# Layer 0's projection of a graph-attention kernel: raw rows with the mean taken out of the weights, weights on another queue, a written-out VectorE order, and the first adjacency block in two transfers

## The chip, the cores and the metric

The kernel runs on one core of a Trainium2 chip. The core has five engines that run side by side and meet through semaphores: TensorE (PE, with its weight loads as PEld), VectorE (DVE), ScalarE (ACT), GpSimd (POOL) and SyncE (SP). SP, ACT and POOL issue DMA transfers, which all share the same 16 DMA engines. The metric is the device time of one execution in microseconds (us); lower is better.

## The reference, cut to what matters

Inputs are 3327 rows of 256 float32 features and a 3327 x 3327 int32 adjacency with entries 0 or 1. Two layers follow one another. In layer 0 the rows are normalised and go through graph attention with two heads, then through a mixture of 16 experts (the best two for each row). In layer 1 they go through graph attention with one head, then through 30 steps of a recurrence. Only the start of layer 0 is touched by the change in substance:

```python
def _layernorm(x, axis=-1, eps=1e-5):
    m, v = jnp.mean(x, axis, keepdims=True), jnp.var(x, axis, keepdims=True)
    return (x - m) / jnp.sqrt(v + eps)

h   = _layernorm(x)
W1h = h @ W1.T + b1;  W2h = h @ W2.T + b2;  W3h = h @ W3.T + b3      # two heads of 128 columns
s1  = einsum(W1h, a[:, :128]);  s2 = einsum(W2h, a[:, 128:])          # one number per row and head
e   = leaky_relu(s1[:, None] + s2[None, :], 0.2), minus infinity where adj is 0
x   = x + softmax(e over neighbours) @ W3h
```

Since s1 and s2 are linear in h, the kernel folds W1, W2 and a into four score columns beside the 256 columns of W3, so that one product of a row with a 256 x 260 matrix `wv` gives everything that attention needs. The products of h with `wv` can be written as (x @ wv') / std, where wv' is `wv` with the mean of each column over its 256 rows subtracted: taking the mean out of the weights does the same as taking it out of the rows, and the factor 1/std of a row can be multiplied in at the end.

## The kernel before, in words

Rows are held in 26 tiles of 128 rows; `groups` takes them four at a time (the last group has two). A tile framework (a scheduler) decides the order of the instructions on each engine from the program's order and the dependencies; instructions passed to `tc.keep_in_program_order` keep their order among themselves. DMA waits and buffer reuse become semaphores.

**Start.** SP issues the loads of x, group by group (L77). ACT's queue writes zeros into three DRAM tensors (`lists`, the last rows of `given`, `no_row`; L418 to L421). POOL's queue loads W1, W2, a, the biases and W3 (`once`, L425, and L437). When W1, W2 and a are there, TensorE folds the score columns (L440), VectorE copies them into `wv` (L444), and TensorE folds the bias of the scores (L452).

**Projection** (`project`, called at L479). For every group `normalized` takes the statistics of its tiles on VectorE (`bn_stats` L116, `bn_aggr` L117, variance plus epsilon L119), GpSimd raises it to the power of minus one half (`rstd`, L121), and VectorE writes the normalised rows `xn` (L128). For each pair of tiles TensorE transposes the four 128 x 128 blocks (L148), ScalarE copies them out of PSUM as `hT` (L149), and one pair later TensorE multiplies them with `wv` (L163, four products of 260 columns). VectorE moves each tile's result out, adding b3 (L459) and the score bias (L463). After each group ScalarE makes three exponentials of the scores and VectorE a negated copy `minus` (L195 to L198). PSUM tiles come from a ring of four banks that transposes and products share.

**Adjacency.** `take_graph` brings in a block of rows of the adjacency. A DMA on POOL's queue reads int32 from DRAM and writes bytes to a DRAM scratch `in_bytes` (L325); for each 128-row tile of it SP then issues a DMA transpose into `adjT` in SBUF (L335). `in_bytes` has room for six tiles and every block starts at its beginning, so that the next block's load waits until the transposes of the one before it are done. The first block has four tiles (`groups0[0]`) and is asked for when the statistics of the fourth group are known (`first_rows`, L473 to L477); POOL issues it behind that group's `rstd`.

**Attention** (`attend`). For one block of target rows and one head at a time, 26 steps run over the source tiles. In each step ScalarE makes `e` (L276), VectorE masks it with `adjT` to `pT` (L281), and TensorE accumulates `pT` with `wh` (L286). A step needs the adjacency of all tiles of its block, so the first step needs all four tiles of the first block. The first two passes (two heads) use 512 columns, those of the second block 768. Ahead of them TensorE spreads the row factors (`rb`, L243) and transposes them all (L224). Routing, the experts, layer 1's attention and the recurrence follow.

Of the kernel before, what the change touches and what calls it, by code (L numbers as in the profile page):

```python
# [21 lines left out]
P = 128  # L22
ALPHA = 0.2
EPS = 1e-5
# [7 lines left out]
def gat_moe_gat_recurrent_ffn(ctx: ExitStack, tc: tile.TileContext, a: dict, out: bass.AP):  # L32
# [77 lines left out]
    def inverse(src, scale=1.0):  # L110

        n = len(src)
        mv = small.tile([P, MOST, 2], F32, name="mv")
        for j in range(n):
            st = small.tile([P, 6], F32, name="st")
            nc.vector.bn_stats(st, src[j])  # L116
            nc.vector.bn_aggr(mv[:, j, :], st)  # L117
        ve = small.tile([P, MOST], F32, name="ve")
        nc.vector.tensor_scalar(ve[:, :n], mv[:, :n, 1], EPS, 1.0 / scale**2, op0=ALU.add, op1=ALU.mult)  # L119
        r = small.tile([P, MOST], F32, name="rstd")  # L120
        power = nc.gpsimd.tensor_tensor(r[:, :n], ve[:, :n], neg_half[:, :n], ALU.pow)  # L121
        return r, mv, power.ins

# [9 lines left out]
    def without_mean(wv, n_out, ones, p):  # L133

        for k in range(KD):
            nc.tensor.matmul(p[:, :n_out], lhsT=ones, rhs=wv[:, k, :], start=(k == 0), stop=(k == KD - 1))
        for k in range(KD):
            nc.vector.scalar_tensor_tensor(
                wv[:, k, :], p[:, :n_out], -1.0 / D, wv[:, k, :], op0=ALU.mult, op1=ALU.add
            )  # L140
# [11 lines left out]
    def project(groups, wv, n_out, finish, work, ps, ps_p, aside, raw=True):  # L152

        pending = None

        def products(hT, t, r):
            for j in range(2):  # L160
                p = ps_p()
                for k in range(KD):
                    nc.tensor.matmul(  # L163
                        p[:, :n_out], lhsT=hT[:, j, k, :], rhs=wv[:, k, :], start=(k == 0), stop=(k == KD - 1)
                    )
                finish(t + j, p, *([r[:, j : j + 1]] if raw else []))

        for ts in groups:
            n = len(ts)
            tiles = [x[:, t, :] for t in ts]  # L170
            if raw:
                r, _, power = inverse(tiles)
            else:
                xn = work.tile([P, G, D], F32, name="xn")
                power = normalized(tiles, [xn[:, j, :] for j in range(n)])
            aside(ts, power)
            for j0 in range(0, n, 2):
                hT = turned(x[:, ts[j0] : ts[j0] + 2, :] if raw else xn[:, j0 : j0 + 2, :], work, ps)
                if pending:
                    products(*pending)  # L180
                pending = hT, ts[j0], r[:, j0 : j0 + 2] if raw else None
        products(*pending)

    class Scores:
# [9 lines left out]
        def finish(self, t0, t1):  # L194
            nc.scalar.activation(self.full[:, t0:t1], self.s[:, t0:t1, 1], AF.Exp)  # L195
            nc.scalar.activation(self.part[:, t0:t1], self.s[:, t0:t1, 1], AF.Exp, scale=ALPHA)
            nc.scalar.activation(self.row[:, t0:t1], self.s[:, t0:t1, 0], AF.Exp, scale=1.0 - ALPHA)
            nc.vector.tensor_scalar(self.minus[:, t0:t1], self.part[:, t0:t1], -1.0, None, op0=ALU.mult)  # L198
# [111 lines left out]
    def take_graph(ts, behind):  # L310
# [6 lines left out]
        b = in_bytes  # L317
# [65 lines left out]
    with ExitStack() as moe:  # L383
# [28 lines left out]
        with ExitStack() as pre:  # L412
# [3 lines left out]
            zero = hold.tile([P, E * CAP * 2 // P], F32, name="zero")  # L416
            nc.vector.memset(zero, 0.0)
            nc.scalar.dma_start(lists.rearrange("(p n) k -> p (n k)", p=P), zero)  # L418
            for k in range(2):
                nc.scalar.dma_start(given[k * NP + N : (k + 1) * NP, :], zero[: NP - N, :D])  # L420
            nc.scalar.dma_start(no_row, zero[:2, : NP // 4])  # L421

            def once(name, shape, src):
                t = hold.tile(shape, F32, name=name)
                nc.gpsimd.dma_start(t, src)  # L425
                return t

            w1 = once("gw1", [P, H, D], a["W1"].rearrange("(h c) d -> c h d", c=P))
            w2 = once("gw2", [P, H, D], a["W2"].rearrange("(h c) d -> c h d", c=P))
            aT = once("gaT", [P, 2, H], a["aT"].rearrange("(s c) h -> c s h", c=P))  # L430
            b1 = once("gb1", [P, H], a["b1"])
            b2 = once("gb2", [P, H], a["b2"])
            b3 = once("gb3", [P, D], every_partition(a["b3"], D))
# [3 lines left out]
            nc.gpsimd.dma_start(wv[:, :, :D], a["W3T"].rearrange("(k p) c -> p k c", p=P))  # L437
            pv = bank()
            for q, (s, h, k) in enumerate((s, h, k) for s in range(2) for h in range(H) for k in range(KD)):
                nc.tensor.matmul(  # L440
                    pv[:, q : q + 1], lhsT=(w1, w2)[s][:, h, k * P : (k + 1) * P], rhs=aT[:, s, h : h + 1],
                    start=True, stop=True,
                )
            nc.vector.tensor_copy(  # L444
                wv[:, :, D:].rearrange("p k q -> p q k"), pv[:, : 2 * H * KD].rearrange("p (q k) -> p q k", k=KD)
            )
            shift = hold.tile([P, 2, H], F32, name="shift")
            nc.vector.memset(shift, 0.0)
            pv = bank()
            for h in range(H):  # L450
                for s, b in ((0, b1), (1, b2)):
                    nc.tensor.matmul(  # L452
                        pv[:, h : h + 1], lhsT=b[:, h : h + 1].to_broadcast([P, P]), rhs=aT[:, s, h : h + 1],
                        start=(s == 0), stop=(s == 1),
                    )
            nc.vector.tensor_copy(shift[:, 0, :], pv[:, :H])

            def split0(t, p):
                nc.vector.tensor_tensor(  # L459
                    wh[:, t, :, :C], p[:, :D].rearrange("p (h c) -> p h c", h=H),  # L460
                    b3.rearrange("p (h c) -> p h c", h=H), ALU.add,
                )
                nc.vector.tensor_tensor(  # L463
                    sc.s[:, t], p[:, D : D + 2 * H].rearrange("p (s h) -> p s h", h=H), shift, ALU.add
                )
                if t % G == G - 1 or t == NT - 1:
                    sc.finish(t - t % G, t + 1)

# [4 lines left out]
            def first_rows(ts, power):  # L473
                nonlocal behind
                behind = power
                if ts is groups[3]:
                    take_graph(groups0[0], behind)  # L477

            project(groups, wv, D + 2 * H, split0, work, ps, bank, first_rows, False)  # L479
# [184 lines left out]
        nc.vector.tensor_copy(vec[:, 0:1], part[:E])  # L664
# [5 lines left out]
        def find_tiles(end, s0, n):  # L670
# [40 lines left out]
            nc.vector.tensor_scalar(vec[:, 1:2], part[:E], float(CAP), None, op0=ALU.mult)  # L711
# [298 lines left out]
    with ExitStack() as st:  # L1010
# [33 lines left out]
        def split1(t, p, r):  # L1044
            nc.scalar.activation(s_wh[:, t, 0, : D + 2], p[:, : D + 2], AF.Copy, scale=r)
            for ts in groups1:
                if t == ts[-1]:
                    sc.finish(ts[0], t + 1)

# [223 lines left out]
```

## Time and profile before

| | us |
|---|---|
| median of 3 runs | 1819.82 |
| lowest, highest | 1819.78, 1823.14 |
| the profiled execution's own time | 1820.76 |
| span of that execution's trace | 1819.0 |

| engine | busy us | share of the span | instructions |
|---|---|---|---|
| PE | 1764.8 | 97% | 10768 |
| PEld | 1608.8 | 88% | 10768 |
| DVE | 1303.0 | 72% | 3861 |
| ACT | 1214.2 | 67% | 1557 |
| POOL | 916.2 | 50% | 702 |

All later readings come from the one profiled execution; its times count from the start of the span. In lines of the timeline the first number is the start, the second the duration of a merged run of equal instructions, xN their number, and the bracket is the idle time of that engine just before, with what ended it. In lines of waits the numbers are the total, how often, and the longest. float32 products appear as two records each[...], so that eight records of L163 are the four products of one pair of tiles.

### The profile page before, as it was taken

Reading aid. Unit: us, or ns where it says so; the run is one execution under the profiler, and the core shown is the slowest. Engines: PE = TensorE matmul, PEld = TensorE weight load, DVE = VectorE, ACT = ScalarE, POOL = GpSimd, SP = SyncE. Lnnn points to the kernel's source line nnn. Section 1 sums busy time; section 2 is a strip of 40 time slices with the busy share of each in tenths; the row PEclk is TensorE's granted clock in tenths of the full one; section 3 lists DMA queues with packets and bytes.
Section 4 is the critical chain, followed back from the end, with each engine's and each line's share of the span. In section 5 each row is a group of like instructions: output and inputs, shape, how many; then the busy total and the mean of one; then the engine's idle time right before and its main releaser. Section 6 shows DMA issues by size and latency. Waiting matters only on the chain.

```text
span 1819.0 us, 32184 instructions
## 1 busy us (share of the span) xinstructions
PE 1764.8 (97%) x10768; PEld 1608.8 (88%) x10768; DVE 1303.0 (72%) x3861; ACT 1214.2 (67%) x1557; POOL 916.2 (50%) x702
## 2 busy tenths in 40 slices
PE   6999999999999999799999999999999999999997
PEld 6999999899999999688888878888888888888885
DVE  7888888863222222657677678889899988998997
ACT  2877677642212121456666579999999999999993
POOL 3011212155454542101111028999999999999993
PEclk9999999999999999899999999999999999999999
DMA  8996360247796875400000038888877888878778
GB/s 174 121 126 81 78 102 10 72 161 211 239 257 192 212 205 163 154 14 18 18 21 16 12 103 188 199 195 199 198 198 192 194 194 196 198 198 201 196 191 233
DMA packets 497026, 269.75 MB, mean 148 GB/s; under 512 B 361797, under 2 KB 469116, under 8 KB 496858
## 3 DMA queue, kind: packets, MB, share of 16 engines
q1 hardware_dynamic: 478722, 229.29, 50.6%
q0 software_dynamic: 13456, 33.60, 10.7%
q10 hardware_dynamic: 4680, 4.76, 0.8%
q8 instruction: 88, 1.44, 0.3%
q14 instruction: 80, 0.66, 0.1%
HBM read 168.19 MB, written 105.58 MB: 151 GB/s over the span
## 4 chain that ended last, share of the span: by engine, by line
PE 54%; DVE 3%; DMA 1%; issue 0%; ACT 0%; SPq 0%; POOL 0%; ACTq 0%; DVEq 0%; POOLq 0%
PE po L1181 36%; PE acc L286 15%; PE bank L1145 3%; DVE pT L281 1%; PE acc L163 1%; DMA old<-kept 1%; DVE x L1030 0%; DMA given<-wh,to 0%; DMA zT<-given 0%; DVE x L1199 0%; DVE x L1191 0%; DVE st L116 0%; POOL rstd L121 0%; DVE low L1064 0%; SPq L1168 0%
## 5 line engine op out<-in xcount | busy, mean ns | idle before, releaser
L276 ACT ACTIVATE e<-rb,minus,full 128x384 f32<-128x384 f32 (+3 forms) x494 | 399.3, 823 | 167.4 <-DVE pT L281 149.6
L1181 PE MATMUL po<-wc,adjT 128*128 128x256 f32 x2144 | 480.0, 380 | 7.5 <-DMA adjT<-apart 5.5
L1115 POOL TENSOR_TENSOR th<-th,x 128x1024 f32<-128x1024 f32 (+1 forms) x210 | 464.7, 2213 | 17.4 <-ACT th L1112 15.7
L281 DVE SCALAR_TENSOR_TENSOR pT<-e,part,adjT 128x384 f32<-128x384 f32 (+3 forms) x494 | 383.5, 782 | 118.4 <-PE acc L286 102.4
L1181 PEld LDWEIGHTS po<-wc,adjT 128*128 128x128 f32 x2144 | 405.9, 191 | 63.5 <-issue 4.9
L1191 DVE SCALAR_TENSOR_TENSOR x<-po,rr,bb 128x256 f32<-128x256 f32 x780 | 323.7, 476 | 73.4 <-PE po L1181 72.8
L286 PE MATMUL acc<-wh,pT 128*128 128x129 f32 x2704 | 310.4, 276 | 2.1 <-DVE pT L281 2.1
L286 PEld LDWEIGHTS acc<-wh,pT 128*128 128x128 f32 x2704 | 305.3, 192 | 2.9 <-DVE pT L281 2.7
L286 PE MATMUL acc<-s_wh,pT 128*128 128x257 f32 x1352 | 295.5, 381 | 4.0 <-DVE pT L281 4.0
L286 PEld LDWEIGHTS acc<-s_wh,pT 128*128 128x128 f32 x1352 | 255.8, 190 | 43.1 <-DVE pT L281 7.4
L1124 DVE BATCH_NORM_STATS2 stats<-z 128x6 f32<-128x256 f32 x780 | 274.4, 412 | 1.4 <-ACT z L1119 1.4
L1156 ACT COPY adjT<-z 128x1024 int16<-128x1024 int16 x268 | 266.9, 1039 | 2.1 <-DVE pT L281 2.0
L1132 POOL TENSOR_TENSOR rr<-v,neg_half 128x4 f32<-128x4 f32 (+1 forms) x210 | 205.6, 979 | 94.2 <-DVE v L1127 88.9
L121 POOL TENSOR_TENSOR rstd<-ve,neg_half 128x4 f32<-128x4 f32 (+3 forms) x28 | 31.9, 1141 | 409.4 <-DVE ve L119 325.6
L1112 ACT ACTIVATE th<-x 128x1024 f32<-128x1024 f32 (+1 forms) x210 | 208.8, 994 | 41.5 <-DVE x L1191 37.7
L1181 PE MATMUL po<-wc,zT 128*128 128x256 f32 x976 | 220.8, 379 | 0.1
L1119 ACT ACTIVATE z<-th 128x1024 f32<-128x1024 f32 (+1 forms) x210 | 209.0, 995 | 6.5 <-POOL th L1115 6.4
L1181 PEld LDWEIGHTS po<-wc,zT 128*128 128x128 f32 x976 | 182.9, 190 | 24.0 <-DVE x L1191 0.5
L931 ACT ACTIVATE e<-bank 128x512 f32<-128x512 f32 x61 | 36.4, 597 | 239.0 <-issue 184.8
L939 DVE TENSOR_TENSOR pT<-e,bank 128x512 f32<-128x512 f32 x61 | 41.9, 687 | 180.3 <-PE bank L881 160.1
L903 POOL DMA_INDIRECT given<-wh,to x61 | 61.1, 1001 | 114.5 <-DVE wh L902 100.0
L594 POOL DMA_INDIRECT lists<-pair,ati x52 | 63.1, 1214 | 107.8 <-DVE ati L581 50.0
(204 smaller groups left out, 1648.0 us busy)
## 6 DMA issues: line engine op xcount, KB each, us to landing
apart<-adjT SPq DMA_DIRECT2D x268, 256.0 KB
wh<-in_w_dram SPq DMA_DIRECT2D x120, 512.0 KB
first_set<-in_w_dram SPq DMA_DIRECT2D x63, 512.0 KB
in_bytes<-in_adj_dram POOLq DMA_DIRECT2D x3, 2496.0 KB
asked<-e POOLq DMA_DIRECT2D x42, 128.0 KB
adjT<-apart SPq DMA_TRANSPOSE x268
x<-in_x_dram SPq DMA_DIRECT2D x6, 512.0 KB
kept<-x SPq DMA_DIRECT2D x8, 384.0 KB
```

The lines of the kernel that those rows point to most:

```text
L276: nc.scalar.activation(e[:, : n * P], rb[:, : n * P], AF.Relu, scale=sc.full[:, j, h : h + 1], bias=sc.minus[:, j, h : h + 1],)
L281: masked = nc.vector.scalar_tensor_tensor(pT[:, : n * P], e[:, : n * P], sc.part[:, j, h : h + 1], adjT[:, j // 2, ts[0] * P : (ts[-1] + 1 ...
L286: nc.tensor.matmul(po[c], lhsT=pT[:, c * P : (c + 1) * P], rhs=wh[:, j, h, :], start=(j == 0 and c % per_bank == 0), stop=(j == NT - 1), s ...
L594: put = nc.gpsimd.indirect_dma_start(out=lists, out_offset=bass.IndirectOffsetOnAxis(ap=ati[: rows(t), s, j : j + 1], axis=0), in_=pair[: ...
L1112: self.put(nc.scalar.activation(self.th, self.hs, AF.Tanh, scale=1.0 / S))
L1115: self.put(nc.gpsimd.tensor_tensor(self.th, self.th, self.hs, ALU.add))
L1119: self.put(nc.scalar.activation(self.z, self.th, AF.Silu, scale=1.0 / S))
L1124: self.put(nc.vector.bn_stats(stats[:, j, :6], self.z[:, j, :]))
L1132: nc.gpsimd.tensor_tensor(self.r[:, : self.n], self.v[:, : self.n, 1], neg_half[:, : self.n], ALU.pow)
L1156: self.put(nc.scalar.copy(parts[:, c : c + 2], halves[:, c : c + 2]))
L1181: nc.tensor.matmul(self.po[:, j, :], lhsT=self.zT(j, k), rhs=wc[:, k, :], start=(k == 0), stop=(k == KD - 1),)
L1191: nc.vector.scalar_tensor_tensor(self.hs[:, j, :], self.po[:, j, :], self.r[:, j : j + 1], bb, op0=ALU.mult, op1=ALU.add)
```

## The change

- `project` transposes x itself for layer 0 too; `xn` and its 26 instructions (L128) are gone. The mean is taken out of `wv` (`without_mean`: two products with a matrix of ones, two VectorE instructions). The exit of each tile multiplies by `rstd` and adds b3 or the score bias in one instruction each.
- The statistics become a generator, `inverting`, that yields after each tile. Group 0 is measured first, then come the score columns, and between their two parts the first two tiles of group 1. All later groups are measured one tile after each exit. The VectorE instructions of this stage are kept in program order.
- ACT's queue loads a, W1, W2 and W3 as its first four transfers. POOL's queue keeps b1, b2 and b3. The zeros go to SP's queue, behind the loads of x.
- TensorE begins with eight products of ones that nobody reads (`idle`).
- The first adjacency block is asked for when group 2's statistics are known, as two loads of two tiles, each with its own place in `in_bytes` and its own two transposes. POOL's small loads and index patterns (`gate_w`, `gate_b`, the iotas) come ahead of it in POOL's order; in the kernel before they came behind it.
- `minus` is made by a separate `negate`, two tiles after the group's end; two small copies of the routing (`vec`) are kept in program order. In the later stages the built programs differ otherwise only in the places of small statistics on VectorE and of two small products.

In the changed program's order TensorE runs: the eight idle products, the transposes of pair 0, the score columns, the products with ones, the bias products, the transposes of pair 1, then the products of pair 0, the transposes of pair 2, and so on. On VectorE group 2's last statistics and its variance stand behind the exit of the fifth tile.

```diff
-    def project(groups, wv, n_out, finish, work, ps, ps_p, aside, raw=True):
+    def project(groups, wv, n_out, finish, work, ps, ps_p, aside, prepare=None):
...
-                finish(t + j, p, *([r[:, j : j + 1]] if raw else []))
+                finish(t + j, p, r[:, j : j + 1])
+                next(ahead, None)
...
+        for g, ts in enumerate(groups):
+            if g == 0 or not prepare:
+                for _ in measure(ts):
+                    pass
+            r = ready.popleft()
+            for j0 in range(0, len(ts), 2):
+                hT = turned(x[:, ts[j0] : ts[j0] + 2, :], work, ps)
                 if pending:
                     products(*pending)
+                elif prepare:
+                    next(prepare)
+                    for j, _ in enumerate(measure(groups[1])):
+                        if j == 1:
+                            next(prepare)
+                    ahead = measure_all(groups[2:])
+                pending = hT, ts[j0], r[:, j0 : j0 + 2]
...
-    def take_graph(ts, behind):
+    def take_graph(ts, behind, base=0):
-        b = in_bytes
+        b = in_bytes[base * P : (base + len(ts)) * P, :]
...
+            aT = once(nc.scalar, "gaT", [P, 2, H], a["aT"].rearrange("(s c) h -> c s h", c=P))
+            w1 = once(nc.scalar, "gw1", [P, H, D], a["W1"].rearrange("(h c) d -> c h d", c=P))
+            w2 = once(nc.scalar, "gw2", [P, H, D], a["W2"].rearrange("(h c) d -> c h d", c=P))
...
+            nc.scalar.dma_start(wv[:, :, :D], a["W3T"].rearrange("(k p) c -> p k c", p=P))
...
+            idle = bank()
+            for _ in range(8):
+                nc.tensor.matmul(idle[:, :P], lhsT=ones, rhs=ones, start=True, stop=True)
...
+                without_mean(wv, D + 2 * H, ones, bank(), tc.keep_in_program_order)
...
-                nc.vector.tensor_tensor(
-                    wh[:, t, :, :C], p[:, :D].rearrange("p (h c) -> p h c", h=H),
-                    b3.rearrange("p (h c) -> p h c", h=H), ALU.add,
-                )
+                tc.keep_in_program_order(
+                    nc.vector.scalar_tensor_tensor(
+                        wh[:, t, :, :C], p[:, :D].rearrange("p (h c) -> p h c", h=H), r,
+                        b3.rearrange("p (h c) -> p h c", h=H), op0=ALU.mult, op1=ALU.add,
+                    )
+                )
...
-                if ts is groups[3]:
-                    take_graph(groups0[0], behind)
+                if ts is groups[2]:
+                    for t in groups0[0][::2]:
+                        behind = take_graph(range(t, t + 2), behind, t)
```

## The prediction, on record before the changed kernel ran

> **What bounds the kernel now.** I read the page first: PE is busy 97% of the span, so what counts is the time in which it stands still. The waits of the first 60 us say where; the timeline of that stretch says when; the DMA view gives the adjacency's pace; the table of stages says who is full.
>
> ```profile
> PE 1764.8 (97%) x10768; PEld 1608.8 (88%) x10768; DVE 1303.0 (72%) x3861; ACT 1214.2 (67%) x1557; POOL 916.2 (50%) x702
> PE bank L440 <- DMA gaT<-in_aT_dram: 12.0, 1, 12.0
> POOL in_bytes L325 <- DMA adjT<-in_bytes: 17.0, 1, 17.0
> ```
>
> PE does nothing for 12 us until W1, W2 and a have landed through POOL's queue.
>
> ```profile
> 12.04 3.54 PE L440 MATMUL bank<-gaT,gw 128*128 128x1 f32 x16 [12.04 <-DMA gaT<-in_aT_dram]
> 16.61 1.01 POOL L121 TENSOR_TENSOR rstd<-ve,neg_half 128x4 f32<-128x4 f32 x1 [0.63 <-DVE ve L119]
> 17.17 1.05 DVE L128 TENSOR_SCALAR xn<-x,mv,rstd 128x256 f32<-128x256 f32 x3
> 17.57 0.92 POOL L325 DMA_DIRECT2D in_bytes<-in_adj_dram  x1
> 20.59 3.56 PE L163 MATMUL bank<-wv,hT 128*128 128x260 f32 x8
> 24.42 1.92 PE L163 MATMUL bank<-wv,hT 128*128 128x260 f32 x8
> 46.35 3.67 PE L163 MATMUL bank<-wv,hT 128*128 128x260 f32 x16
> 48.24 0.77 POOL L325 DMA_DIRECT2D in_bytes<-in_adj_dram  x1 [16.95 <-DMA adjT<-in_bytes]
> 51.16 2.22 PE L243 MATMUL bank<-ident,row 128*128 128x128 f32 x18
> 53.30 2.95 PE L286 MATMUL acc<-wh,pT 128*128 128x129 f32 x24
> ```
>
> The first xn starts at 17.17 although its rstd was there at 8.0, because VectorE ran the statistics of later groups first. Products run from 20.59 to 50.02, a pair every 2.19 us once under way; the first pT follows at 52.50. Beside this chain runs another: the adjacency, asked for at 17.57. The next load of in_bytes may start only when its transposes are done, so 48.24 is the latest moment at which it was there: 30.7 us after the request, and 4.3 us before it was needed. That slack limits the change.
>
> ```profile
> 20.60:50.00 29.40, 29.40 (x151) 25.39 (x151) 21.97 (x97) 8.95 (x30) 4.68 (x14) 1.00 0.85 116
> 52.50:101.80 49.30, 49.30 (x442) 49.18 (x442) 43.07 (x65) 45.96 (x60) 0.69 (x1) 1.00 0.94 116
> ```
>
> PE is full in both stages (first figure behind the length), so a microsecond won or lost before the first pT should reach the end.
>
> **The change part by part.**
>
> *Weights on ACT's queue.* Before, ACT's queue waited for the memset of the zeros until 2.36. Now it can begin with SP, at 0.8. x shows the delay: issued at 0.80, 0.52 MB moved by 4.0, first statistics at 4.72. The three matrices are 0.77 MB. x moves in 2 KB packets, rows of the weights are 1 KB; if the queues take turns by packet, the weights get a third of some 345 GB/s from about 2.9 on: W2 is complete after 1.57 MB, at 7.5, W3 after 2.36 MB, at 9.7; with 0.6 for the landing 8.1 and 10.3. Against 12.04 that is the first gain. x itself gets no more and no fewer bytes to share with, and the zeros behind it on SP delay only the transposes, which are far later. POOL's three small loads have no work behind them that is late.
>
> *Until the first product.* Idle products, transposes of pair 0 and the W1 columns fit before 8.1. Eight W2 records at 0.22 (3.54/16) end by 9.9; the copy, ready by 10.3, does not bind. The products with ones: layer 1's same step takes 1.15 from its first product (728.44) to its first correction on VectorE (729.59), so 10.4 to 11.5; the two corrections take 0.77 (there 0.76). Meanwhile PE does eight bias records (at 0.11, the spacing of L243 and L286, to 12.4) and pair 1's transposes (0.60). First product: 13.0, 7.6 earlier than 20.59. Bounds: 12 if W3 gets an equal share, 15.5 if PE is still slow (below).
>
> *Projection.* Transposes and products stay; xn goes (26 instructions by 0.35 on VectorE, which is not the bound). The exit is one instruction with a scalar more; L138 (the same kind, from PSUM) takes 0.42, L459 0.42: nothing. VectorE per pair: two exits 0.83, two statistics 0.82, some 0.2 of small ones: 1.85 below PE's 2.19, so the written order fits; a statistic stands in front of an exit for 0.4, which the four banks cover. PE's stage is 29.43 less the slow start (3.56 - 1.92 = 1.64): 27.8. It ends at 40.8, and with before's tail of 2.48 the first pT could come at 43.3.
>
> *The adjacency's request* does not come earlier. It waits for group 2's rstd, which in VectorE's new order stands behind the fifth tile's exit. Fifth product: 2 x 2.19 + 0.81 = 5.2 after the first one, wait and exit 0.6, statistics and variance 0.3, handover 0.15, power 1.01: 7.3. Request at 20.3, against 17.57. POOL has nothing else waiting there: the small loads and iotas moved ahead of it took 18.48 to 21.8 in before and now lie between two powers, from about 8 on.
>
> *Two halves.* In before: request to first bytes 1.6, load 16.8 (19.2 to 36), landing and start of the transposes 2.7, transposes 38.7 to 47.2, landing about 1. The transposes' work, by their share of the engines:
>
> ```profile
> q1 hardware_dynamic: 1781, 0.45, 49.9%
> q1 hardware_dynamic: 3478, 0.87, 109.5%
> q1 hardware_dynamic: 1525, 0.38, 53.3%
> ```
>
> (three windows of 4 us, 37 to 49) is 2.0 + 4.4 + 2.1 = 8.5 us of all engines. While the load runs its queue holds 103 to 104% of them, so the trace has no idle engine under which half one's transposes could vanish. [...] By that rule the sum stays 1.6 + 16.8 + 8.5 + 1 = 28: only the gap of 2.7 is filled. By a hope that they overlap fully it would be 26.4; if halves share evenly and the gap opens again behind half two, 30.7. I take 28. The adjacency is there at 48.3.
>
> *First pT*: the later of 43.3 and 48.3, plus 0.1: 48.4 against 52.50. **Gain 4.1 us.** The next load is asked for at the same time as before (48.3 to 48.24), so its transposes end near 92.2 as before, while its first use moves from 101.8 to 97.7: covered, by 5.5. The later blocks have more.
>
> *A new idle stretch on PE.* After products end at 40.8 the row factors take 3.4 more as before (50.02 to 53.38), to 44.2; the first attention product comes at 49.2. PE, which went without a break, now idles for 5 us. What that costs is seen elsewhere:
>
> ```profile
> 739.29 1.12 PE L148 MATMUL bank<-ident,x 128*128 128x128 f32 x4 [7.76 <-DVE x L1030]
> 741.12 3.38 PE L163 MATMUL acc<-wv,hT 128*128 128x258 f32 x8 [0.72 <-ACT hT L149]
> 745.62 2.45 PE L163 MATMUL acc<-wv,hT 128*128 128x258 f32 x10 [0.24 <-ACT hT L149]
> ```
>
> After 7.76 idle the same products take almost double for about 5 us (3.38 for eight against 1.92: 1.5, and 0.5 in the transposes: 2.0 lost). After 1.82 idle (L136 at 728.44) they ran at full pace. The granted clock in the table is 1.00 throughout and doesn't show it. [...] I take nothing for the number, 2.0 for the range.
>
> **The sum.** Profiled execution: 1820.76 (span 1819.0 and 1.76 around it), less 4.1: 1816.7. The median of the runs lies 0.94 below that execution, so 1815.7.
>
> **Rivals.**
> - *Half speed after the idle stretch.* As above, with 2.0 back: gain 2.1, 1817.7. For it: the 7.76 row; against it: the stretch is shorter.
> - *The overlap is better, or the start is earlier.* W3 by 9.3 puts the request at 19.3; transposes hidden: 26.4 and pT at 45.8. Gain 6.7, 1813.1; with no adjacency wait at all 52.5 - 43.3 = 9.2, 1810.6. Against it: the load's 103%.
> - *Late request, slower than before.* If the idle products fail to bring PE to speed (16 records of L440 in a row, 12.04 to 15.58, did not; L163 at 20.59 was still slow), the products with ones, the bias and pair 1's transposes double: first product at 15.5, the first eight products and the transposes cost 1.7 more, request at 24.5. With halves that share evenly, 30.7 more: 55.2, first pT 2.8 later than before, and a slow restart adds 2.0: 4.8 slower, 1824.6. It decides from a request at 52.4 - 28 = 24.4 on, or 21.7 with even sharing. Against it: idle products and transposes keep PE busy from 1.5 to about 7.
> - *The change does nothing for the time*: products earlier, the adjacency again at 50 to 52: gain under 2, 1818.8.
>
> **How the numbers follow.** About 0.2% (3.6 us) is what a measurement of this kernel can tell from no change; the three runs differ by 3.4. Main case 0.42 (its own range 2.6 to 5.6, two thirds above 3.6); half speed 0.25; better overlap 0.20; nothing 0.06; slower 0.07. Faster by over 0.2%: 0.28 + 0.20 = 0.48; slower 0.07; within 0.45. The range leaves out the ends of the second and third rival: 1811.6 to 1821.0.
>
> **What would show it.** In the changed profile: first product near 13, request near 20.3 as two L358 issues, transposes of half one in the queue before half two has landed, the last pair near 40.8, first pT at 48.4 with a wait on a DMA of adjT, and behind it PE records of L319 at 0.11 or 0.22. Wrong if the request comes before 18 or after 23, if the wait before the first pT is on anything but the adjacency, or if the second block's first step waits.

## The result and the profile after

The changed kernel takes 1829.41 us (median of 6 runs, 1828.87 to 1832.61) where the kernel before took 1820.16 in the same session (6 runs, 1819.13 to 1823.14): ratio 1.0041, 95% interval 1.0029 to 1.0054. It is slower by 0.4%; the forecast was 1815.7, and the range ended at 1821.0. The profiled execution of the changed kernel took 1829.29, with a span of 1827.6.

The waits of its first 60 us, in the columns used above (total, times, longest):

```profile
PE bank L475 <- DMA gw<-in_W_dram: 3.9, 2, 2.3
DVE pT L314 <- DMA adjT<-in_bytes: 6.4, 1, 6.4
PE acc L319 <- DVE pT L314: 5.4, 1, 5.4
```

The 12 us in which PE waited for the weights have become two waits of 3.9 together, as the change wants. But 6.4 us of waiting for the adjacency have appeared ahead of the first pT, where there was none. The timeline says how:

```profile
7.68 1.02 PE L475 MATMUL bank<-gaT,gw 128*128 128x1 f32 x8 [1.59 <-DMA gw<-in_W_dram]
11.05 1.86 PE L475 MATMUL bank<-gaT,gw 128*128 128x1 f32 x8 [2.35 <-DMA gw<-in_W_dram]
15.44 1.71 PE L490 MATMUL bank<-gaT,gb 128*128 128x1 f32 x8
17.89 3.67 PE L178 MATMUL bank<-wv,hT 128*128 128x260 f32 x8
27.87 1.22 POOL L358 DMA_DIRECT2D in_bytes<-in_adj_dram  x2
44.51 3.67 PE L178 MATMUL bank<-wv,hT 128*128 128x260 f32 x16
56.30 2.08 DVE L314 SCALAR_TENSOR_TENSOR pT<-e,part,adjT 128x512 f32<-128x512 f32 x3 [6.37 <-DMA adjT<-in_bytes]
56.45 0.75 POOL L358 DMA_DIRECT2D in_bytes<-in_adj_dram  x1 [13.46 <-DMA adjT<-in_bytes]
```

The first product comes at 17.89, only 2.7 us before 20.59. The request for the adjacency goes out at 27.87 instead of 17.57: 10.3 later. From it to the adjacency, for which the first pT at 56.30 waited, it takes 28.4 us; in the kernel before it was 30.7, read at the next load of in_bytes. So the adjacency is 8.1 later than before; 4.3 us of that was slack, and the first pT is 3.8 later (56.30 against 52.50), although the last products end 1.8 earlier.

The table of stretches (length; PE busy; then the other engines; granted clock third from the end, DMA share next to last):

```profile
8.00:12.00 4.00, 1.65 (x12) 1.57 (x11) 0.00 (x0) 0.00 (x0) 3.08 (x18) 0.66 0.94 335
12.00:24.00 12.00, 11.34 (x40) 9.77 (x40) 5.25 (x21) 1.17 (x2) 1.03 (x1) 0.54 0.41 133
24.00:47.70 23.70, 23.70 (x130) 20.65 (x129) 20.05 (x88) 7.78 (x28) 5.92 (x7) 1.00 0.82 82
57.00:62.00 5.00, 4.89 (x29) 4.89 (x30) 3.10 (x6) 3.37 (x5) 0.20 (x1) 0.65 0.87 81
```

Between 8 and 12 PE works 1.65 us and loses its clock (0.66 there, 0.50 from 9.3 to 22.9 us); from 12 to 24 it is busy 11.34 of 12 us at about half speed (the same step of PE, eight bias records, takes 1.71 here and 0.95 in the run below that keeps PE at full clock). Behind the wait for the adjacency the clock is low once more (0.65). Instruction by instruction against the kernel before, attention's first product is 3.8 us late, and the products once attention is under way are 5.4 late: this restart costs another 1.6.

### The profile page after: what moved, and what is told of

Read it like the earlier page. It is cut to its first block, busy times and chain, and to the rows that moved or that the text cites. A ratio compares the mean times of both kernels' runs of the same rounds, so it can differ in the third digit from the quotient of the medians.

```text
span 1827.6 us, 32199 instructions
## 1 busy us (share of the span) xinstructions
PE 1775.2 (97%) x10788; PEld 1618.8 (89%) x10788; DVE 1298.2 (71%) x3837; ACT 1215.2 (66%) x1557; POOL 912.0 (50%) x699
## 4 chain that ended last, share of the span: by engine, by line
PE 80%; DVE 6%; DMA 6%; issue 4%; POOL 2%; ACT 1%; SPq 1%; ACTq 0%; DVEq 0%; POOLq 0%
PE po L1239 35%; PE acc L319 28%; PE bank L938 7%; PE acc L955 3%; DVE pT L314 3%; PE bank L1203 3%; DMA given<-wh,to 2%; PE acc L178 1%; PE bank L163 1%; DMA wh<-in_w_dram 1%; DMA in_bytes<-in_adj_dram 1%; PE bank L583 1%; POOL given L960 1%; DMA old<-kept 1%; SPq L368 1%
## 5 line engine op out<-in xcount | busy, mean ns | idle before, releaser
L319 PEld LDWEIGHTS acc<-s_wh,pT 128*128 128x128 f32 x1352 | 257.0, 191 | 43.6 <-DVE pT L314 7.3
```

Of the source, the lines that this page charges most:

```text
L319: nc.tensor.matmul(po[c], lhsT=pT[:, c * P : (c + 1) * P], rhs=wh[:, j, h, :], start=(j == 0 and c % per_bank == 0), stop=(j == NT - 1), s ...
```

## The experiments

Every run is compared with the kernel before, timed beside it on the same chip; its median there was 1824.8, 1826.4, 1824.8 and 1820.8 in the four sessions, so that differences count and absolute times do not. The first product is that of `wv`, the request is the first adjacency load on POOL's queue, the first pT is the first masked tile of attention; all three, in us, come from one profile of each run. "Start" is how much later than in the first profile of the kernel before PE works once attention is under way (at 100 us); it holds the first pT and the restart. In the two other profiles of the kernel before it is -0.3 and +0.4. A half-clock stretch is one in which the granted clock of the profile reads 0.50.

| kernel | first product | request | first pT | start | median less before's |
|---|---|---|---|---|---|
| before | 20.59 | 17.57 | 52.50 | 0 | 0 |
| changed | 17.89 | 27.87 | 56.30 | +5.4 | +9.3 |
| changed, again | 17.63 | 27.52 | 55.38 | +4.5 | +7.0 |
| request one group earlier | 17.53 | 19.20 | 49.83 | -2.7 | +0.6 |
| PE kept busy before attention | 17.56 | 26.93 | 54.61 | +1.9 | +6.0 |
| PE kept busy at the start | 16.04 | 23.52 | 51.45 | +1.5 | +3.1 |
| weights on SP | 16.64 | 25.21 | 53.62 | +3.7 | +5.9 |
| weights on SP, request earlier | 16.55 | 18.23 | 47.96 | -4.5 | +0.5 |
| b3 behind x | 17.27 | 26.01 | 54.12 | +4.3 | +7.9 |
| one request | 17.61 | 26.57 | 58.52 | +8.7 | +10.4 |
| norms in old order | 18.07 | 26.54 | 54.75 | +4.9 | +7.0 |
| all together | 14.23 | 16.32 | 48.38 | -4.1 | -4.4 |
| all together, again | 13.99 | 16.07 | 45.63 | -6.9 | -2.9 |
| ... with the changed norm order | 13.42 | 15.51 | 44.89 | -7.6 | -4.6 |
| ... with b3 behind group 1 | 14.14 | 16.23 | 44.36 | -8.1 | -5.8 |
| ... and vec free | 14.23 | 16.32 | 44.46 | -8.0 | -5.2 |

**Is the late request the cause?** In the changed kernel only the place of the request moves:

```diff
-                if ts is groups[2]:
+                if ts is groups[1]:
```

> The changed kernel, with the adjacency asked for behind the variance power of group 1 instead of group 2; nothing else moves. Late-request theory (the request at 27.87 us, behind the fifth tile's exit, used up the 4.3 us of slack): request near 19.7 us, adjacency there 28.4 us later at 48.1, first pT then bound by the products' end (48.2 + 2.5) at about 50.8 instead of 56.30, no cold start of PE behind it, time 1818 to 1821 us, about 8 to 10 us below the changed kernel. Rival, the halves cost: request to adjacency stays above 31 us and the first pT comes after 52.5. Rival, raw projection and the written order cost later on: first pT earlier as said, but the end no more than 3 us below the changed kernel.

```profile
19.20 1.22 POOL L358 DMA_DIRECT2D in_bytes<-in_adj_dram  x2
46.45 0.75 POOL L358 DMA_DIRECT2D in_bytes<-in_adj_dram  x1 [4.25 <-DMA adjT<-in_bytes]
49.83 12.65 DVE L314 SCALAR_TENSOR_TENSOR pT<-e,part,adjT 128x512 f32<-128x512 f32 x15 [0.68 <-ACT e L309]
```

The adjacency is there 27.3 us after the request, and pT waits for ACT, not for a DMA. Request, first pT and the missing restart came as the late-request theory said: where the changed kernel loses 7 to 9 us to the kernel before, this one loses 0.6 (ratio 1.0005, 0.9995 to 1.0015). So neither the halves nor the written order is the main loss. But the start is now 2.7 us early and the end is not; some 3 us are lost behind it.

**What is the restart worth?** 20 idle products between the projection and the row factors:

```diff
+            idle = bank()
+            for _ in range(20):
+                nc.tensor.matmul(idle[:, :P], lhsT=ones, rhs=ones, start=True, stop=True)
```

> The changed kernel with 20 further idle products of ones by ones on PE (about 4.4 us) between the last layer-0 product and the row factors; their result is used nowhere. They fill most of the 5.45 us in which PE waits for the adjacency. Theory of the clock: first pT stays at 56.3, granted clock behind it 1.00 instead of 0.63, first 768-column pT at about 105.6 instead of 107.23, time about 1.6 us below the changed kernel (1827.8). Rival, the first products there are slow for lack of pT and not for the clock: nothing changes (1829.4).

```profile
47.08 4.63 PE L531 MATMUL bank<-ones 128*128 128x128 f32 x40
55.42 8.75 PE L319 MATMUL acc<-wh,pT 128*128 128x129 f32 x76 [0.48 <-DVE pT L314]
```

```profile
55.40:60.00 4.60, 4.58 (x41) 4.58 (x42) 4.17 (x6) 4.49 (x7) 0.11 (x1) 1.00 0.85 80
```

The clock behind the wait is 1.00 instead of 0.65, and PE goes from 2.1 us late at its first attention product to 1.9 once under way, where the changed kernel goes from 3.8 to 5.4. In the runs that kept the wait the restart took 1.6 (both profiles of the changed kernel) to 2.7 us. (The first pT is 1.7 earlier than expected; 0.9 of this is the request, which was that much earlier in this execution.) The times are too close for a verdict on 1.6 us: 1.0034 (1.0022 to 1.0047).

**Why was the first product so late?** Two candidates: PE's clock, and the weights' landing. First 22 more idle products in the gaps ahead of the first real ones:

```diff
+                fill(6)                                  # ahead of W1's columns
...
+                    if (s, h, k) == (1, 0, 0):
+                        fill(11)                         # between W1's and W2's
...
+                fill(5)                                  # ahead of the products with ones
```

> The changed kernel with 22 more idle products of ones by ones on PE: 6 ahead of the columns of W1, 11 between those of W1 and W2, 5 ahead of the products of ones by W3. Theory that of the 4.9 us by which the first product missed its forecast (17.89 against 13.0) about 2 are PE's half clock and 3 the late landing of W2: W2's columns begin at 11.05 as before, the step after them runs at full pace (bias 0.85 instead of 1.71, first eight products 1.92 instead of 3.67), first product 15.5 to 16, request 25.0 to 25.5 instead of 27.87, first pT 53.5, time 2.5 to 3 us below the changed kernel. Rival, the clock does not follow from the gaps: first product 17.9, nothing changes.

```profile
11.87 0.95 PE L482 MATMUL bank<-gaT,gw 128*128 128x1 f32 x8
14.75 0.95 PE L498 MATMUL bank<-gaT,gb 128*128 128x1 f32 x8
16.04 1.92 PE L178 MATMUL bank<-wv,hT 128*128 128x260 f32 x8
23.52 1.22 POOL L358 DMA_DIRECT2D in_bytes<-in_adj_dram  x2
51.45 2.08 DVE L314 SCALAR_TENSOR_TENSOR pT<-e,part,adjT 128x512 f32<-128x512 f32 x3 [5.87 <-DMA adjT<-in_bytes]
```

```profile
8.00:12.00 4.00, 3.56 (x32) 3.59 (x33) 0.00 (x0) 0.00 (x0) 3.18 (x18) 1.00 1.04 369
12.00:16.00 4.00, 4.00 (x35) 3.88 (x34) 1.93 (x8) 0.00 (x0) 0.00 (x0) 1.00 1.07 344
```

With the clock at 1.00 the way from W2's columns to the first product takes 4.2 us instead of 6.8, and from the first product to the request 7.5 instead of 10.0. The fillers themselves hold W2's columns back by 0.8. The request gains 4 us where 2.5 had been expected, and the time follows: 3.1 above before, against 7.0 for the changed kernel on the same chip. That chip's run of it:

> The changed kernel unaltered, to be compared in one session with the experiments beside it and with the kernel before. It should again lie about 0.4% above the kernel before. Theory of a clock grid (a PE gap of some 1.9 us costs one stretch of 3.4 us at half clock when it falls wholly into one stretch of a grid that is not tied to the program's start): first pT within 0.5 us of 56.3 as before, but the single half-clock stretches (at 347.2, 736.3 and 784.1 in the first profile) at other places. Rival, these stretches belong to the program: the same stretches again.

It gave 1.0045 (1.0028 to 1.0061) and a first pT at 55.38, 0.9 from that of the first run where 0.5 had been expected; of the single half-clock stretches named, those at 347.2 and 736.3 were missing and that at layer 1's attention came again (790.5); what the profiles show around such stretches stands in the last section.

Then the landing. Weights behind x's first group on SP's queue:

```diff
-    for ts in groups:
+    for ts in groups[:1]:
...
+            for ts in groups[1:]:                        # behind aT, W1, W2, W3, all on nc.sync
```

> The changed kernel with aT, W1, W2 and W3 moved from ACT's queue to SP's, behind x's first group and ahead of its others, so that they no longer share with all of x. Theory that the weights' late arrival let PE lose its clock and so moved every later step: W2 there by 7 us instead of 11.05, first product near 12 instead of 17.89, granted clock 1.00 from 8 to 24, request near 20 to 21, first pT 48 to 49 instead of 56.3, time 1816 to 1819 us. Rival, VectorE's written order alone sets the request (statistics of groups 1 and 2 then wait for x): first product earlier, request not before 25, first pT above 53, time 1825 or more.

W1's columns ran at 6.34, but W2's still at 10.15 and the clock was lost all the same (the eight bias records took 1.71 once more); first product 16.64, request 25.21. A miss: the queue alone wins 1 us. With the earlier request too:

> Both edits together: weights on SP's queue behind x's first group, adjacency asked for behind group 1's power. If the two causes add: first product near 12, request near 15, adjacency there at 43.5, products end near 40, first pT at about 43.6, time 1811 to 1815 us, below the kernel before (1820). If the load of the adjacency now starves x and delays the later groups: last product after 44 and first pT after 47.

First product (16.55) and end of the last products (45.52) are again later than expected, and the first pT is at 47.96, not 43.6, with the adjacency there since 45.57. These are the numbers of the rival, but not its cause: from the first product to the end of the last one it takes 29.0 us here and 28.9 in the run before, whose request came 7 us later, so the early load starves nobody; the products end late because they begin late. The time stays at 1.0002 (0.9994 to 1.0010) of that of the kernel before.

What else was on the DMA engines while W2 was late? Queues in the changed kernel from 7 to 9 us (packets, MB, share of 16 engines; q10 carries the weights, q0 POOL's small loads, q1 SP's x):

```profile
q0 software_dynamic: 63, 0.13, 51.2%
q1 hardware_dynamic: 109, 0.22, 32.3%
q10 hardware_dynamic: 107, 0.11, 15.6%
```

Half of the engines' time went to b3, one row of 1 KB copied to every partition: 32 packets of 0.51 us each on average in this profile (0.28 us, and 33.5% of the engines, in the second profile of the same kernel). Moved behind x:

```diff
-            b3 = once(nc.gpsimd, "gb3", [P, D], every_partition(a["b3"], D))
+            b3 = once(nc.sync, "gb3", [P, D], every_partition(a["b3"], D))
```

> The changed kernel with only the load of b3 (one row of 1 KB written to every partition, 32 packets of about 0.5 us) moved from POOL's queue to SP's, behind x. Theory that these packets held half of the engines from 7 to 9 us in front of W2 and x: W2's columns begin at about 10 instead of 11.05, first product about 1 us earlier (16.9), request 1 us earlier (26.9), first pT 55.3. Rival, the weights are late because they share with x, and b3 is nothing: W2 at 11.

```profile
q1 hardware_dynamic: 224, 0.43, 59.4%
q10 hardware_dynamic: 219, 0.21, 34.8%
q0 software_dynamic: 26, 0.00, 1.4%
```

In the same two microseconds twice the bytes of weights and x move, and W2's last packet is there at 9.36 instead of 10.05. Yet W2's columns run at 10.70, only 0.35 earlier (in the six profiles with the changed kernel's start they run between 10.84 and 11.20): b3 was worth about a third of what was expected. Its ratio, 1.0049 (1.0031 to 1.0067), is that of the changed kernel.

**The two halves.** The first adjacency in one request at the same place:

```diff
-                    for t in groups0[0][::2]:
-                        behind = take_graph(range(t, t + 2), behind, t)
+                    behind = take_graph(groups0[0], behind)
```

> The changed kernel with the first adjacency asked for whole, in one request at the same place, instead of in two halves. Request at 27.5 to 27.9 us as in the changed kernel. If the halves are worth what the prediction took for them (they fill the gap of 2.7 us between load and transposes): adjacency there 30.7 us after the request instead of 28.0 to 28.4, first pT 58.4 to 58.8 instead of 55.4 to 56.3. Rival, the halves cost time, since the second half waits behind the first one's transposes: request to adjacency under 28 us.

```profile
26.57 0.71 POOL L358 DMA_DIRECT2D in_bytes<-in_adj_dram  x1
58.52 2.08 DVE L314 SCALAR_TENSOR_TENSOR pT<-e,part,adjT 128x512 f32<-128x512 f32 x3 [9.90 <-DMA adjT<-in_bytes]
```

From the request to the first pT 31.9 us, against 27.7 to 28.4 with halves in all the kernels of the table that waited for it. The halves are worth at least 3.5 us here (the single request of the kernel before took 30.0 to 30.7 us in its three profiles), and are no part of the loss. They do not work by overlap: from 42 to 46 us in the changed kernel the load (q0) fills the engines, and the transposes of half one (q1) get what is left. So the gap that they fill is what remains; it was 2.7 us in the kernel before, and where the rest of the 3.5 comes from is not shown.

```profile
q0 software_dynamic: 127, 0.42, 100.7%
q1 hardware_dynamic: 100, 0.03, 4.4%
```

**The loss behind the start.** Over the table the end is on average 2.8 us later than the start tells (from 0.3 less to 5.0 more). Two parts of the change also move VectorE's order behind layer 0: `inverting` sets each tile's aggregate behind the next tile's statistics, in every layer norm, and two writes of `vec` in the gate are held in program order. The norms first:

> The changed kernel with every layer norm outside layer 0's projection given back its old order on VectorE (aggregate of a tile directly behind its statistics, instead of one tile later). Theory that the new order costs about 0.44 us at the end of the first attention (five statistics instead of four behind the last row, a PE gap of 1.86 instead of 1.42 us) and a few tenths more behind it: first pT unchanged at 55.4 to 56.3, PE gap near 345 back at 1.42, time 0.5 to 1 us below the changed kernel, too little for the comparison of times to show. Rival: gap stays 1.86.

The gap stayed at 1.85: the rival. Then everything together, to see whether a clean start reaches the end:

> What the other runs found, put together: weights on SP's queue behind x's first group; b3 behind x; 17 more idle products on PE ahead of the first real ones; adjacency asked for behind group 1's power; layer norms in their old order. Expected: first product 13.5 to 14.5, no half clock at the start, request 15 to 16, adjacency there at 43.5 to 44.5, last product at 43.5 to 44.5, first pT near 45.5 to 46.5 without a long PE gap ahead of it, 6 to 7 us earlier than in the kernel before (52.5), time 3 to 6 us below the kernel before. If a gain at the start does not reach the end (as in the two runs with an early request): within 1 us of the kernel before.

```profile
14.23 1.92 PE L181 MATMUL bank<-wv,hT 128*128 128x260 f32 x8
19.48 1.12 PE L181 MATMUL bank<-wv,hT 128*128 128x260 f32 x4 [2.02 <-DVE s L518]
```

```profile
18.72 0.49 DVE L512 SCALAR_TENSOR_TENSOR wh<-bank,rstd,gb 128x256 f32<-128x256 f32 x1 [3.48 <-DMA gb<-in_b_dram]
```

Faster than before: 0.9970 (0.9961 to 0.9979). The expectation missed one thing: the first exit waited 3.5 us for b3, now too late; PE stood 2.0 us and lost its clock once more (0.79 from 16 to 24). Three variants follow, beside a second run of it:

> The version with everything together, unaltered, as the reference of the three beside it. Again about 0.3% below the kernel before (ratio 0.997), first pT at 48.4, with the PE gap of 2.0 us near 17.5 where the first exit waits for b3.

It gave 0.9985 (0.9974 to 0.9996), 1.5 us less of a gain for the same kernel; the gap was 1.19 this time, no half-clock stretch followed, and the first pT came at 45.63. With the changed order of the norms:

> The same, but with the changed kernel's order of statistics and aggregates in every layer norm. In the runs so far the end was about 3 us later than the start of attention accounts for where this order was in (seven kernels), and about 0 where it was not (two). If the order costs that: about 3 us above the version together, with no single place in the trace that takes it. Rival, those 3 us are the scatter of the executions: no difference beyond 1 us.

0.9977 (0.9967 to 0.9988), 1.7 us below the run beside it: the order of the norms does not cost the 3 us. With b3 earlier:

> The version together, with b3 moved on SP's queue from behind all of x to behind x's second group. The first exit no longer waits for it: the PE gap of 2.0 us near 17.5 goes and the half-clock stretch behind it (20.7 to 24.1) as well, last product 2 to 3.5 us earlier, first pT at 45 to 46.4 instead of 48.4, time 2 to 3 us below the version together. Rival: b3's slow packets in front of x delay group 2's statistics, and the gain is under 1 us.

```profile
14.14 1.92 PE L181 MATMUL bank<-wv,hT 128*128 128x260 f32 x8
16.23 1.22 POOL L361 DMA_DIRECT2D in_bytes<-in_adj_dram  x2
43.78 0.75 POOL L361 DMA_DIRECT2D in_bytes<-in_adj_dram  x1 [7.05 <-DMA adjT<-in_bytes]
44.36 18.01 DVE L317 SCALAR_TENSOR_TENSOR pT<-e,part,adjT 128x512 f32<-128x512 f32 x21 [0.68 <-ACT e L312]
```

PE's wait for b3 and the half-clock stretch behind it are gone: 0.9971 (0.9961 to 0.9980), 5.8 us below the kernel before, with the first pT 8.1 earlier. Its median is the lowest; those of the variant before it and of the next lie within 1.2 us of it, less than the intervals tell apart. Last, with `vec` free as well:

> As with b3 earlier, and the two writes of vec in the gate no longer held in program order, so that VectorE's order behind layer 0's projection is the one of the kernel before throughout. PE gap near 336 to 340 at 1.42 instead of 1.85 us, 0.4 us on the path; with it one fewer chance of a half-clock stretch there (1.7 us in the runs that had one). Time 0.4 to 1.5 us below the run with b3 earlier. Rival: gap still 1.85, no difference.

In the profile of the version with b3 earlier, and then in that with vec free:

```profile
332.93 3.08 PE L322 MATMUL acc<-wh,pT 128*128 128x129 f32 x16 [1.86 <-DVE pT L317]
```

```profile
332.98 2.05 PE L322 MATMUL acc<-wh,pT 128*128 128x129 f32 x16 [1.41 <-DVE pT L317]
```

So the held `vec` moves a set of statistics from under PE's work to the end of the first attention: 0.44 us, and here a half-clock stretch on top. Such a stretch followed this gap in 8 of the 14 changed profiles that had it, and costs half a microsecond more, not 1.7, since it takes the place of PE's next wait of 1.08 us: from this gap to the one of 0.69 us behind it that every profile has, it takes 13.5 us in the first of these two profiles, 12.5 in the second, and 13.0 with the gap but no stretch (the second run of everything together). In the times it does not show: 0.9972 (0.9959 to 0.9984).

Is the rest inside the first attention too? From 100 us to its last product the changed kernel and the experiments on it (ten profiles) are 0.5 to 3.4 us slower than the first profile of the kernel before, the five profiles of everything together and its variants 0.0 to 1.0. Beside `vec` and its stretch the traces show another half-clock stretch near 350 to 356 us in two of the ten (1.65 us), and a wait of PE of some 0.3 us near 370 in seven. Two more profiles of the kernel before show what moves by itself:

> The kernel before unaltered, for a second profile beside those of the experiments. First pT near 52.5. Clock grid theory: layer 1's projection start is slow again (the gap of 7.76 us holds two whole stretches), and the gap of 1.89 us before layer 1's attention (774.3) has about an even chance of a half-clock stretch, which would add 1.7 us. Rival: no half-clock stretch there in the kernel before, whatever the run.

> The kernel before unaltered, a third profile of it, on the chip of the runs beside it. Start phase as in the other two (first product 20.2 to 20.6, first pT 52.2 to 52.5). It shows how far the stage of gate and experts, 337.0 us in the first profile and 344.7 in the second, moves without any change: over 339 again if it belongs to the chip or the execution and not to the change.

From just behind the first attention (391.4 us in the first profile) to layer 1's first products the three executions took 337.0, 344.7 and 339.6 us: inside that stage PE waits, mostly for the experts' rows and weights and the gate's counts, for 1.5, 6.9 and 2.8 us in all. Where layer 1's attention starts, one of the three had a half-clock stretch, two not. Both are no part of the change. In the first attention, from 100 us on, the second and third were 0.7 and 0.1 us slower than the first.

## Why the prediction was wrong

- *What bounds the kernel; the slack of 4.3 us behind the adjacency:* right, and the place where it was decided.
- *Weights on ACT's queue (W2 landing at 8.1, W3 at 10.3):* wrong, the first step that failed. W2's columns ran at 11.05, 3.0 later. The trace gives three parts. The first packet of W1 started at 4.72, not at 2.9, behind the 256 packets of 8 bytes that the load of a makes (3.07 to 4.49): 1.8 us, the largest, put at nothing in the sum. The 0.52 MB of W1 and W2 then took 5.3 us where a third of 345 GB/s gives 4.6: 0.8 us. From the last packet (10.05) to the columns it was 1.0 instead of 0.6: 0.4 us. "POOL's three small loads have no work behind them that is late" overlooked that their packets take engine time from others, but moving b3 wins only 0.35 us. No run moved a, so that its packets are the cause of the late beginning is read from their order and not tested.
- *Until the first product (13.0, bounds 12 to 15.5):* 17.89, outside its bounds: 3.0 from the landing, 1.9 from PE's half clock. The clock was named, in the rival, with "idle products and transposes keep PE busy from 1.5 to about 7" against it. They did so until 6.1, with W1's columns at 7.68; but W2 came at 11.05, and between 5.88 and 9.30, just before the clock fell (1.00 up to 9.30, 0.50 behind it), PE stood for 2.2 us. The argument hung on the landing and fell with it.
- *Request 7.3 behind the first product:* right at full clock (7.5 in the run with PE kept busy), 10.0 as it ran. So the request left at 27.87 and not at 20.3: 4.9 us from the first product, 2.7 behind it, nearly all of this the half clock.
- *Two halves, 28 us:* right: 28.4. No run shows for queues in general that the times of two add up in full, as the sum does with the load's 16.8 and the transposes' 8.5; for these two the runs showed 100.7% of the engines for the load and 4.4% for the transposes beside it, against the hope of overlap. One request took 31.9.
- *Gain 4.1:* became a loss of 3.8 at the first pT; 28.4 added to 27.87 is what the prediction's own sum would have given.
- *The new idle stretch taken at nothing:* mis-sized. PE idled 5.45 us and the restart took 1.6, in other runs up to 2.7; without the idle stretch nothing. The row behind 1.82 us of idle had no loss, that behind 7.76 lost 2.0; the forecast put its 5.0 with the first, and the loss behind 5.45 came out near the second. "The granted clock in the table is 1.00 throughout and doesn't show it" holds for the two stretches printed there, but at the row it argues from, behind 7.76 us of idle, the profile of the kernel before does show the half clock:

```profile
735.00:740.00 5.00, 0.71 (x4) 0.71 (x4) 2.36 (x6) 0.00 (x0) 0.00 (x0) 0.50 0.95 297
740.00:745.00 5.00, 4.28 (x16) 3.22 (x16) 4.70 (x11) 0.60 (x2) 0.00 (x0) 0.60 1.08 351
```

- *Late request, slower than before (0.07):* this is what happened. "It decides from a request at 24.4 on" was right: with requests at 25.2, 26.0 and 26.5 the first pT is later than before, and with 23.5 it comes 1 us before 52.5 (that run is still slower by 3.1, since it pays the restart). It was given too little, since its case against rested on one landing time.
- *A microsecond before the first pT reaches the end:* nearly. Over the 15 runs of the table, with starts from -8.1 to +8.7, the end follows the start about one to one, but some 2.8 us late. Of this 0.44 is the held `vec`, with 0.5 more where a half-clock stretch follows; a run excludes the norm order as the cause of 3 us. The rest is not settled: part of it lies in the first attention, where half-clock stretches come and go from profile to profile, and the stage of gate and experts differs by up to 7.7 us between executions of the kernel before.

## What to carry to other kernels

When a request is moved behind a step of another engine, its time is that step's time: work out at which landing, and at which clock, the moved request falls behind its slack, before counting the gain on the other path. A step that arrived in pieces (weights, then compute, then weights) cost TensorE its clock here (0.50 from 9.3 to 22.9 us), and its instructions on the way to the request then took nearly double (1.71 against 0.95 us for the bias records); idle products in those gaps cost 0.8 us and won 4 at the request. Ask for the long transfer at the first moment that does not starve the short ones: here that, a PE kept busy, b3 out of the way and the weights behind x's first rows together made the loss of 0.4% a gain of 0.3%.

## What the runs showed of the hardware

- In the first profile of the changed kernel the granted clock reads 0.50 from 9.30 us for 13.65, from 53.67 for 6.83, from 347.22 for 3.41, from 736.34 for 3.41, from 743.16 for 10.24, from 784.12 for 3.41, and in the last 2.4 us; in that of the kernel before from 733.71 for 10.24, from 1805.49 for 3.41, and in the last 3.3. All but the two that the end cuts off last one to four times 3.41 us. From the span's start they begin at a multiple of 3.4133 us plus 2.47 in the one profile and plus 3.26 in the other. In the 3.41 us ahead of the six PE was idle for 2.19, 2.01, 1.85, 2.23, 3.41 and 2.22 us; ahead of the two, for 2.18 and 2.38.
- In 18 profiles PE stands for 1.88 us before layer 1's attention, and for 0.34 us a little earlier. Behind it 3.41 us at half clock followed in 12 of them, and none in 6: the attention's first 21 records took 6.51 us in the first profile of the changed kernel, the first 20 took 4.60 in the third of the kernel before. In steps of 3.41 us counted on from the changes of the clock, PE's idle time in the step that holds most of the gap was 2.22 in the first of these two profiles, 2.00 in the second run of everything together, 1.65 in the third profile of the kernel before and 1.51 in its first; half clock followed in the first two of these four and not in the last two. No run varies this gap alone, so what decides it is not shown. This step and the next, in the second run of everything together and in the third profile of the kernel before (PE's busy time stands behind the length):

```profile
767.68:771.10 3.42, 1.42 (x10) 0.98 (x8) 1.23 (x4) 2.67 (x8) 0.00 (x0) 1.00 0.04 8
771.10:774.51 3.41, 3.18 (x8) 2.54 (x9) 1.50 (x4) 2.52 (x5) 0.00 (x0) 0.50 0.09 30
```

```profile
775.67:779.08 3.41, 1.76 (x11) 1.29 (x9) 0.89 (x4) 2.65 (x8) 0.00 (x0) 1.00 0.02 3
779.08:782.50 3.42, 2.85 (x13) 2.53 (x14) 2.33 (x4) 3.38 (x6) 0.00 (x0) 1.00 0.18 58
```

- The record of the granted clock begins at 23.7 us in the first profile of the kernel before and at 5.9 in that of the changed kernel, and what lies ahead of it reads as 1.00: the kernel before ran its first eight products, from 20.59 on, in 3.56 us instead of 1.92 under a clock of 1.00. In these two profiles a 1.00 ahead of 23.7 and 5.9 is therefore no reading.
- One row copied to all partitions, beside the loads of x and of the weights, moved in 32 packets of 4 KB, whose mean was 0.51 us in one execution of the changed kernel and 0.28 in another (the least was 0.16): 51% and 33.5% of all DMA engines for 2 us.
